# Five edits to the order of a macaron block's kernel: branches, bias splits, a scheduling fence, placement sums and the attention's instruction order

## The chip, the cores and the metric

The kernel runs on one core of a Trainium2 chip. A core has TensorE (PE, with its weight loads listed as PEld), VectorE (DVE), ScalarE (ACT), GpSimd (POOL) and SyncE (SP), which work side by side and wait for each other by semaphores; DMA queues are fed by SP, ACT and POOL. The metric is the device time of one launch in microseconds (us); lower is better.

## The reference

All data is fp32; `x` is (4, 1024, 256). A block of three residual parts is computed:

```python
x = x + 0.5 * ffn(layernorm(x))
x = x + attn(layernorm(x))      # 16 heads; k and v from a 128-wide latent; rope; mask by pages of 64
x = x + 0.5 * ffn(layernorm(x)) # the same weights again

def fff(x, nw, nb, w1, b1, w2, b2, act):      # 256 leaves of width 16, tree of depth 8
    node = 0
    for _ in range(8):
        node = 2 * node + 1 + ((x . nw[node]) + nb[node] > 0)
    leaf = node - 255
    return act(x @ w1[leaf] + b1[leaf]) @ w2[leaf] + b2[leaf]

def ffn(x):
    xn = (x - mean(x)) / sqrt(std(x) + 1e-5)
    q, k, v = (fff(xn, ..., relu) for each of three weight sets)
    y = xn + softmax(q k^T / sqrt(256)) v      # one head, per batch of 1024 tokens
    return y + fff(y, ..., gelu)               # the fourth set, f
```

So each ffn holds four fast feed-forward trees (q, k, v, f) and a single-head attention between v and f.

## The kernel before, in words

The 4096 tokens are 32 tiles of 128. A tree goes through these steps. **Routing** (`route`, `routes`): PE transposes tiles of `xn` (L317), multiplies with all node weights (L326), DVE compares with thresholds `thr` (`bits`, L334), and PE and ACT turn the bits into one-hot leaves. **Placement** (`place`, `ranks`, `blocks_ended`): the 256 leaves form 32 blocks of 8. A token's slot in a list sorted by block is worked out, each block padded to whole tiles; `blocks_ended` adds up how many tiles each block has with small matmuls, L439, L447 and L465, with short DVE chains between them. **Scatter** (`scattering`, `go`): POOL writes each token's row to its slot in DRAM, one indirect DMA a tile (L554). **Build** (`load_first`): a w1 load `raw` is transposed on PE (L615) and copied to its tile by ACT (L620) and DVE (L618, half of the pieces for q, k and v). **Leaves** (`leaves`): for each of up to 63 tiles SP loads 128 sorted rows `xg` (L656); PE transposes them (L662), multiplies with its block's w1 (L680), adds the bias by a matmul with `b1p` (L683), DVE masks the leaf (L688), PE transposes again (L698) and multiplies with w2 (L705). The first 48 tiles are always done; the rest stand behind three nested run-time branches in `spare_leaves` (L641), which each engine takes by itself.

`b1p` is the bias b1 in three bf16 parts. `load_raw` loads b1 three times on SP's queue (L589) ahead of the w1 loads, and `split_b1` makes the parts with seven DVE operations: one copy (L597), three subtractions (L601) and three copies (L602). Both are called once for each tree in each ffn.

Side work is written as generators, which `with_steps`, `beside` or the due times (`at`, `due`) of the single-head attention move on, one step after each leaf tile, routing group or score step. k is placed beside q's leaves and v beside k's leaves. f is routed and placed beside the single-head attention, in three runs of tiles (`in_runs`, called by `place_run(k, n)` for n steps of run k), and its rows are settled there (L1055). q's placement is drained in one go.

A scheduler of the framework orders each engine's instructions by its own estimate of when they are ready, except inside `in_order()`, where they stay in source order. `tc.keep_in_program_order` pins single DMAs. The w2 load of v is issued on ACT's queue (L572) behind k's branches, which no instruction is moved across, and v's w1 is built right behind it; then `coming` gathers rows of k and q (`y_k` and `b_k`, POOL, L739 and L753), DVE adds them (L972) and PE turns them, beside v's leaves.

The 16-head attention runs 16 units of 12 steps (four batches by four groups of heads). A step has two waves: in each, two heads' scores for the maxima (L1403, reduced by DVE, L1410) and two heads' scores for the weights (L1437, exponentials on ACT, L1444); the weighted sums are L1455. All the scores share a few PSUM banks `big`. Between them, `prepare` makes the next tiles' q, k and v: z (DVE, L1358), its transposes (PE, L288), the latent (L1365), q and k (L1373, L1379), rope on DVE (L1291, L1293) and POOL (L1296, L1298), v's copy `vpad` (ACT, L1381), and the transposes of q and k by heads (L1304) with their copies `qTh` and `kTh` (L1383, L1385). The whole of it is in source order:

```python
es.enter_context(in_order())
```

Of the kernel before, what the change touches and what calls it, by code (L numbers as in the profile page):

```python
# [71 lines left out]
def macaron_kernel(ctx: ExitStack, tc: tile.TileContext, a: dict, out: bass.AP):  # L72
# [33 lines left out]
    def sm(shape):  # L106
        return bank("sm", shape)
# [37 lines left out]
    null = const.tile([P, 1], F32, name="null")  # L145

# [287 lines left out]
    def blocks_ended(pool, acc, t, last=True, k=0, before=()):  # L434
# [11 lines left out]
        pe = sm([NBLK, 1])  # L446
        nc.tensor.matmul(pe, tri[:NBLK, :NBLK], upto[:, :1], start=True, stop=(k == 0))  # L447
        if k:
            nc.tensor.matmul(pe, ones[:NBLK, :NBLK], before[1], start=False, stop=True)
# [5 lines left out]
        nc.vector.tensor_copy(upto[:, 1:], total)  # L455
        end = pool.tile([NBLK, 1], F32, name=f"endc{k}", tag=f"endc{k}")
# [3 lines left out]
        if last:  # L460
            nc.vector.tensor_scalar(past, tiles, end, None, ALU.is_ge)
        else:
            nc.vector.tensor_scalar(past, tiles, end, null[:NBLK], ALU.is_ge, ALU.mult)
        pg = sm([P, GCOL])
        nc.tensor.matmul(pg, ones[:NBLK], past, start=True, stop=True)  # L465
        return pg, (total, upto[:, 1:])
# [10 lines left out]
    def place(pool, oh, acc, rows, gblk, sel):  # L477
# [10 lines left out]
        n, _ = blocks_ended(pool, acc, NT)  # L488
        yield
        tile_blocks(pool, n, end, gblk, sel)  # L490
# [3 lines left out]
    def in_runs(pool, oh, acc, rows, gblk, sel):  # L494
# [9 lines left out]
        def run(k):  # L504
# [30 lines left out]
            n, before = blocks_ended(pool, acc, hi, last, k, before)  # L535
# [49 lines left out]
    def load_raw(pool, f):  # L585

        b1 = pool.tile([3 * NBLK, P], F32, name=f"b1_{FFFS[f]}", tag="b1")
        for k in range(3):
            nc.sync.dma_start(  # L589
                b1[k * NBLK : (k + 1) * NBLK, :],  # L590
                a[f"{FFFS[f]}_b1"].rearrange("(b e) l -> b (e l)", e=EPB),
            )
        return b1, [load_part(pool, f, *p) for p in PART[:2]]

    def split_b1(b1p, b1):

        nc.vector.tensor_copy(b1p, b1)  # L597
        for k in range(1, 3):
            for q in range(k, 3):
                one = slice(q * NBLK, (q + 1) * NBLK)  # L600
                nc.vector.tensor_sub(b1[one], b1[one], b1p[one])  # L601
                nc.vector.tensor_copy(b1p[one], b1[one])  # L602
# [25 lines left out]
    def spare_leaves(*what):  # L628
# [12 lines left out]
        with ExitStack() as es:  # L641
            for lo, hi in zip(SPARE, SPARE[1:]):
                es.enter_context(tc.If(used > lo))
# [155 lines left out]
    def ffn(first: bool, last: bool):  # L799
# [13 lines left out]
        with ExitStack() as es:  # L813
            xn = stage(es, "xnp", 1).tile([P, NT, E + 2], F32, name="xn")
            idx = stage(es, "idx", 1)
            slot, leaf, gblk, sel, b1p = [], [], [], [], []
            for nm in FFFS:
# [4 lines left out]
                b1p.append(idx.tile([3 * NBLK, P], BF16, name=f"b1p_{nm}"))  # L822
# [17 lines left out]
            with ExitStack() as ws, banks(0, 8):  # L840
# [8 lines left out]
                with ExitStack() as hs, ExitStack() as rs:  # L849
                    raw = stage(rs, "raw", 1, "right")  # L850
                    pp = stage(hs, "place", 1)
                    with ExitStack() as rt:
# [38 lines left out]
                        b1, ahead = load_raw(raw, 0)  # L891
                        split_b1(b1p[0], b1)
# [17 lines left out]
                        b1, ahead = load_raw(raw, 1)  # L910
# [10 lines left out]
                        split_b1(b1p[1], b1)  # L921
# [15 lines left out]
                    b1, ahead = load_raw(raw, 2)  # L937
# [12 lines left out]
                    split_b1(b1p[2], b1)  # L950
                    drain(load_first(raw, 2, w1, ahead))

# [54 lines left out]
            b1, raws = load_raw(raw, 3)  # L1007
            with in_order(), qs, ExitStack() as ats, banks(2, 4):
# [169 lines left out]
                drain(weights)  # L1178
                path = route(rp, 3, NT - 1, *hot_f, leaf[3], 1)
# [4 lines left out]
            with ExitStack() as fs, banks(0, 8):  # L1184
                with in_order():
# [53 lines left out]
    def attention():  # L1239
# [7 lines left out]
        with ExitStack() as es:  # L1247
# [73 lines left out]
            es.enter_context(in_order())  # L1321
# [318 lines left out]
```

## Time and profile before

| what | value |
|---|---|
| times of three runs | 2679.99, 2681.26, 2692.75 us; median 2681.26 |
| the profiled execution | 2683.48 us, span 2681.6 us |
| mean granted TensorE clock | 0.952 of full |
| busy share of the span | PE 88%, PEld 56%, DVE 55%, ACT 40%, POOL 32% |
| start and routing of q, first ffn | 0 to 75 us |
| scatter and build of q, routing of k | 75 to 147 us |
| leaves of q; build of k and routing of v | 147 to 222; 222 to 262 us |
| leaves of k; build of v; leaves of v | 262 to 355; 355 to 378; 378 to 470 us |
| single-head attention, then f | 470 to 800; 800 to 897 us |
| 16-head attention | 897 to 1790 us |
| second ffn | 1790 to 2682 us |

The profile page has one execution on the chip. A row of waits reads: engine, tile and line that stood idle, then the engine (or DMA), tile and line that ended the wait, then total us, number of times, and the longest. A row of the timeline reads: start, duration, engine, line, operation, tiles out<-in with sizes, and in brackets the engine's idle time before it and what ended that. A row of one line's instructions ends in shortest/median/longest ns; a q behind an engine's name is its sequencer. Windows give busy times, granted clock and the share of the DMA engines for a stretch of the span. Bounds of the stages above are read from such windows.

### The profile page before, as it was taken

What the parts mean: (1) busy time and instruction counts of PE and PEld (TensorE: products, weight loads), DVE (VectorE), ACT (ScalarE), POOL (GpSimd) and SP (SyncE); (2) the same over time, 40 slices, a digit from 0 to 9 for tenths busy, and PEclk for the clock granted to TensorE, in tenths of its full rate; (3) what the DMA queues carried; (4) which work ended last, traced back from release to release, by engine and by line L of the source; (5) the groups of instructions that cost most, each with busy time, mean ns of one, the idle gap of its engine ahead of it and who ended that gap; (6) DMA issues with size and microseconds to landing.
All of it is one profiled execution on the core that took longest, in us unless ns stands there. A gap on an engine that the chain in (4) does not pass through costs nothing. (4 is left out here: it accounts for less than half of the span.)

```text
span 2681.6 us, 43134 instructions
## 1 busy us (share of the span) xinstructions
PE 2364.6 (88%) x14388; PEld 1511.0 (56%) x14430; DVE 1483.1 (55%) x4401; ACT 1064.1 (40%) x2491; POOL 855.1 (32%) x978
## 2 busy tenths in 40 slices
PE   7789878999988679999999999979999899999874
PEld 3476777566657434434344344435676785666573
DVE  8554544455545475666665667645645454455453
ACT  3334344233224224545554545544443452332241
POOL 0431344466445311101101100003421554664453
PEclk9889989999998779999999999999999899999987
DMA  9966686344226200000000000002656873442265
GB/s 284 334 199 214 205 247 194 123 147 145 66 103 211 89 8 1 1 1 1 1 1 1 1 1 1 2 33 95 227 186 222 267 231 123 144 144 69 97 204 167
DMA packets 236919, 321.22 MB, mean 120 GB/s; under 512 B 28529, under 2 KB 208002, under 8 KB 232584
## 3 DMA queue, kind: packets, MB, share of 16 engines
q1 hardware_dynamic: 150480, 170.24, 20.7%
q0 software_dynamic: 38640, 100.90, 11.9%
q10 hardware_dynamic: 47560, 47.06, 5.4%
q8 instruction: 130, 2.13, 0.3%
q14 instruction: 109, 0.89, 0.1%
HBM read 193.59 MB, written 129.33 MB: 120 GB/s over the span
## 5 line engine op out<-in xcount | busy, mean ns | idle before, releaser
L1410 DVE TENSOR_REDUCE mxh<-big 128x1 f32<-128x512 f32 (+3 forms) x768 | 391.9, 552 | 251.0 <-PE big L1403 248.4
L1444 ACT ACTIVATE pTh<-big 128x512 f32<-128x512 f32 (+3 forms) x768 | 332.7, 489 | 287.8 <-PE big L1403 257.3
L1403 PE MATMUL big<-kTh,qTh 32*128 32x512 f32 (+3 forms) x1536 | 407.3, 541 | 7.7 <-DVE mxh L1410 6.1
L1437 PE MATMUL big<-qTh,kTh 32*128 32x512 f32 (+3 forms) x1536 | 342.5, 534 | 0.1
L326 PE MATMUL sm<-xT,nwT 128*128 128x512 f32 (+2 forms) x528 | 240.1, 598 | 10.1 <-DVE bits L334 7.3
L767 PE MATMUL two<-kT,qT 128*128 128x512 f32 x512 | 237.3, 608 | 10.0 <-ACT pr L780 8.4
L688 DVE SCALAR_TENSOR_TENSOR hm<-eid,xg,sm 128x128 f32<-128x128 f32 x399 | 138.1, 346 | 187.0 <-PE sm L683 185.5
L795 PE MATMUL sm<-vb,pT 128*128 128x256 f32 x1024 | 232.0, 380 | 1.8 <-DVE pT L791 1.8
L707 ACT COPY og<-sm 128x256 f32<-128x256 f32 x399 | 148.7, 373 | 151.4 <-DMA ytok<-og,tok 39.2
L795 PEld LDWEIGHTS sm<-vb,pT 128*128 128x128 f32 x1024 | 190.0, 190 | 28.2 <-DVE pT L791 3.5
L700 ACT ACTIVATE hid<-sm 128x128 f32<-128x128 f32 x399 | 111.3, 279 | 229.0 <-PE sm L698 227.5
L1437 PEld LDWEIGHTS big<-qTh,kTh 32*128 32x128 f32 x1536 | 115.9, 184 | 148.2 <-issue 72.9
L662 PE MATMUL sm<-ident,xg 128*128 128x128 f32 x798 | 161.3, 286 | 25.8 <-DMA xg<-xs_f 18.3
L1403 PEld LDWEIGHTS big<-kTh,qTh 32*128 32x128 f32 x1536 | 156.1, 185 | 42.5 <-ACT pTh L1444 23.4
L664 DVE COPY xgT<-sm 128x256 f32<-128x256 f32 x399 | 166.4, 417 | 21.0 <-PE sm L662 20.1
L1455 PE MATMUL sm<-pTh,vpad 128*32 128x512 f32 (+3 forms) x1536 | 167.3, 499 | 4.7 <-ACT pTh L1444 4.7
L334 DVE TENSOR_SCALAR bits<-sm,thr 128x512 bf16<-128x512 f32 (+1 forms) x132 | 96.8, 734 | 121.7 <-PE sm L326 121.0
L326 PEld LDWEIGHTS sm<-xT,nwT 128*128 128x128 f32 x528 | 98.4, 196 | 114.7 <-issue 87.8
L767 PEld LDWEIGHTS two<-kT,qT 128*128 128x128 f32 x512 | 95.1, 195 | 110.3 <-issue 97.3
L320 ACT COPY xT<-sm 128x512 f32<-128x512 f32 (+1 forms) x130 | 69.7, 582 | 198.7 <-PE sm L317 198.3
L775 DVE TENSOR_REDUCE mx<-two 128x1 f32<-128x1024 f32 x64 | 78.3, 1224 | 125.2 <-PE two L767 125.2
L1419 POOL TENSOR_SCALAR mpad<-mxh 128x16 f32<-128x16 f32 x32 | 8.9, 279 | 390.0 <-DVE mxh L1410 234.8
(322 smaller groups left out, 4413.6 us busy)
## 6 DMA issues: line engine op xcount, KB each, us to landing
xg<-xs SPq DMA_DIRECT2D x298, 128.5 KB
xs<-zero SPq DMA_DIRECT2D x2, 8095.5 KB
xs_f<-zero ACTq DMA_DIRECT2D x14, 1032.0 KB
xg<-xs_f SPq DMA_DIRECT2D x101, 129.0 KB
os_q<-og SPq DMA_DIRECT2D x101, 128.0 KB
os_v<-og SPq DMA_DIRECT2D x101, 128.0 KB
os_k<-og SPq DMA_DIRECT2D x96, 128.0 KB
raw_q<-in_q_w SPq DMA_DIRECT2D x8, 1024.0 KB
```

The lines of the kernel that those rows point to most:

```text
L326: nc.tensor.matmul(pl, nwT[:, c, f, r * P : (r + 1) * P], xT[:, c, :], start=(c == 0), stop=(c == KC - 1),)
L662: nc.tensor.transpose(pa[:, c, :], xg[:, x0 + c * P : x0 + (c + 1) * P], ident)
L664: nc.vector.tensor_copy(xT, pa)
L688: nc.vector.scalar_tensor_tensor(hm, eid, xg[:, lf : lf + 1], ph, ALU.is_equal, ALU.mult)
L707: nc.scalar.copy(og, po)
L767: nc.tensor.matmul(ps[:, n0 : n0 + 512], qT[:, c, i * P : (i + 1) * P], kT[:, c, n0 : n0 + 512], start=(c == 0), stop=(c == KC - 1),)
L795: nc.tensor.matmul(po, pT[:, j, :], vb[:, j, :], start=(j == 0), stop=(j == TPB - 1))
L1403: nc.tensor.matmul(ps[:, :n], qT[r : r + HPAD, hg, i * P : (i + 1) * P], kT[r : r + HPAD, hg, n0 : n0 + n], start=True, stop=True,)
L1410: nc.vector.tensor_reduce(maxima(b, hg)[:, i, c, u : u + 1], ps[:, :n], AX.X, ALU.max)
L1437: nc.tensor.matmul(ps[:, off:], kT[r : r + HPAD, hg, j * P : (j + 1) * P], qT[r : r + HPAD, hg, qb * QN + off : (qb + 1) * QN], start=True ...
L1444: nc.scalar.activation(pT[:, u, off:], ps[:, off:], AF.Exp, scale=1.0 / math.sqrt(HD))
L1455: nc.tensor.matmul(acc[r : r + HPAD, off:], vpads[b % 2][:, j, 4 * hg + 2 * pair + u, :], pTs[pair][:, u, off:], start=(j == 0), stop=(j = ...
```

## The change

There are five edits.

1. `spare_leaves` tells the compiler that the block without work comes next behind the compare. In the program, the small block of the case "not taken" now lies directly behind the compare, and the bodies behind it; before, the bodies came first.
2. b1 is loaded on ACT's queue, and only in the first ffn; its parts `b1p` are kept in the constants for both. The splits are written beside k's routing; the scheduler puts all 28 operations and the 12 loads into q's routing (loads of b_q ahead of and among the `thr` loads, b_k behind them, b_v and b_f among ACT's work at about 45 and 56 us of the old profile).
3. `tc.no_sync_barrier()` behind v's build: the scheduler may not move instructions across that place; nothing waits for it at run time. On DVE the copies of `w_v` now come ahead of the first three adds L972, and on POOL gathers of `y_k` and `b_k` alternate.
4. `blocks_ended` becomes a generator that pauses ahead of each of its two later matmuls, and the calls of `place_run` are spread to match. L447 and L465 of k, v and f come behind a leaf tile, a score step or a build step.
5. In the 16-head attention source order ends with the first unit of 12 steps; the scheduler orders the rest. On PE the score matmuls L1437 come ahead of the transposes of z (L288) in 21 cases; on DVE z (L1358) moves up to 32 reduces earlier; on ACT the copy `vpad` moves behind one or two exponentials in 24 of 32 prepares; on POOL the copies L1298 come ahead of the additions L1296.

The number of instructions on PE and POOL does not change. The diff, with four hunks that only rename left out:

```diff
@@ -143,6 +143,8 @@
 mod32 = const.tile([P, 1], F32, name="mod32")
 null = const.tile([P, 1], F32, name="null")
+b1p = [const.tile([3 * NBLK, P], BF16, name=f"b1p_{nm}") for nm in FFFS]
 with tc.tile_pool(name="nodes", bufs=2) as np_, banks(0, 8):
     nc.vector.memset(nwT[:, :, :, NODES:], 0.0)
@@ -431,7 +433,7 @@
     nc.vector.tensor_scalar_mul(first, first, float(P))
     return first
-def blocks_ended(pool, acc, t, last=True, k=0, before=()):
+def blocks_ended(pool, acc, t, found, last=True, k=0, before=()):
@@ -443,16 +445,17 @@
 ng = tiles_of(pool, n)
 upto = pool.tile([NBLK, 2], BF16, name=f"upto{k}", tag=f"upto{k}")
 nc.vector.tensor_copy(upto[:, :1], ng)
-pe = sm([NBLK, 1])
-nc.tensor.matmul(pe, tri[:NBLK, :NBLK], upto[:, :1], start=True, stop=(k == 0))
-if k:
-    nc.tensor.matmul(pe, ones[:NBLK, :NBLK], before[1], start=False, stop=True)
 total = pool.tile([NBLK, 1], F32, name=f"total{k}", tag=f"total{k}")
...
 nc.vector.tensor_copy(upto[:, 1:], total)
+yield
+pe = sm([NBLK, 1])
+nc.tensor.matmul(pe, tri[:NBLK, :NBLK], upto[:, :1], start=True, stop=(k == 0))
+if k:
+    nc.tensor.matmul(pe, ones[:NBLK, :NBLK], before[1], start=False, stop=True)
 end = pool.tile([NBLK, 1], F32, name=f"endc{k}", tag=f"endc{k}")
 nc.vector.tensor_add(end, pe, ng)
 past = pool.tile([NBLK, GCOL], BF16, name="past_g", tag="past_g")
@@ -461,9 +464,10 @@
         nc.vector.tensor_scalar(past, tiles, end, None, ALU.is_ge)
     else:
         nc.vector.tensor_scalar(past, tiles, end, null[:NBLK], ALU.is_ge, ALU.mult)
+    yield
     pg = sm([P, GCOL])
     nc.tensor.matmul(pg, ones[:NBLK], past, start=True, stop=True)
-    return pg, (total, upto[:, 1:])
+    found += [pg, (total, upto[:, 1:])]
 def tile_blocks(pool, n, end, gblk, sel):
@@ -485,9 +489,10 @@
     for h in range(2):
         yield from ranks(pool, oh, acc, rows, h * NT // 2, (h + 1) * NT // 2, first)
         yield
-    n, _ = blocks_ended(pool, acc, NT)
+    found = []
+    yield from blocks_ended(pool, acc, NT, found)
     yield
-    tile_blocks(pool, n, end, gblk, sel)
+    tile_blocks(pool, found[0], end, gblk, sel)
 RUNS = (0, NT - TPB, NT - GT, NT)
@@ -532,7 +537,9 @@
         pass
     yield
 last = k + 2 == len(RUNS)
-n, before = blocks_ended(pool, acc, hi, last, k, before)
+found = []
+yield from blocks_ended(pool, acc, hi, found, last, k, before)
+n, before = found
 yield
 if k:
     nc.vector.tensor_add(ended, ended, n)
@@ -584,22 +591,24 @@
 def load_raw(pool, f):
-    b1 = pool.tile([3 * NBLK, P], F32, name=f"b1_{FFFS[f]}", tag="b1")
+    return [load_part(pool, f, *p) for p in PART[:2]]
+def load_b1(pool, f):
+    b1 = pool.tile([3 * NBLK, P], F32, name=f"b1_{FFFS[f]}", tag="b1", bufs=2)
     for k in range(3):
-        nc.sync.dma_start(
+        nc.scalar.dma_start(
             b1[k * NBLK : (k + 1) * NBLK, :],
             a[f"{FFFS[f]}_b1"].rearrange("(b e) l -> b (e l)", e=EPB),
         )
-    return b1, [load_part(pool, f, *p) for p in PART[:2]]
-def split_b1(b1p, b1):
-    nc.vector.tensor_copy(b1p, b1)
+    yield
+    nc.vector.tensor_copy(b1p[f], b1)
     for k in range(1, 3):
         for q in range(k, 3):
             one = slice(q * NBLK, (q + 1) * NBLK)
-            nc.vector.tensor_sub(b1[one], b1[one], b1p[one])
-            nc.vector.tensor_copy(b1p[one], b1[one])
+            nc.vector.tensor_sub(b1[one], b1[one], b1p[f][one])
+            nc.vector.tensor_copy(b1p[f][one], b1[one])
+        yield
 def load_first(pool, f, w1, raws, on_both=True):
@@ -640,7 +649,7 @@
 )
 with ExitStack() as es:
     for lo, hi in zip(SPARE, SPARE[1:]):
-        es.enter_context(tc.If(used > lo))
+        es.enter_context(tc.If(used > lo, preferred_fallthrough_block=False))
         for _ in leaves(*what, lo, hi):
             pass
@@ -888,8 +896,7 @@
 if first:
     clear(nc.sync, xs[0])
 w1 = w1_of(0)
-b1, ahead = load_raw(raw, 0)
-split_b1(b1p[0], b1)
+ahead = load_raw(raw, 0)
 if first:
     tc.keep_in_program_order(clear(nc.sync, xs[1]))
 build = load_first(raw, 0, w1, ahead)
@@ -898,16 +905,28 @@
 going = scattering(0, slot[0], rows, 5)
 hot = hots_of(pp, 1, 2)
+if first:
+    b1s = [load_b1(raw, f) for f in range(len(FFFS))]
+    for g in b1s[:2]:
+        next(g)
 def beside(k):
     drain(islice(build, 3 * (k > 0)), islice(going, 1))
+    if first and k and k % 2 == 0:
+        f = k // 2 - 1
+        drain(b1s[f])
+        if f + 2 < len(FFFS):
+            next(b1s[f + 2])
 routes(hp, 1, *hot, leaf[1], beside)
 drain(build, going)
+if first:
+    drain(*b1s)
 w2 = load_second(nc.sync, wp, 0)
...
 what = tree(0, AF.Relu, w1, w2)
-b1, ahead = load_raw(raw, 1)
+ahead = load_raw(raw, 1)
 rows = []
 with_steps(
     leaves(*what),
@@ -947,8 +965,8 @@
         tc.keep_in_program_order(clear(nc.sync, osrt[2][SPARE[0] * P :]))
     w1 = w1_of(2)
     w2 = load_second(nc.scalar, wp, 2)
-    split_b1(b1p[2], b1)
     drain(load_first(raw, 2, w1, ahead))
+    tc.no_sync_barrier()
 early = stage(ws, "early", 2)
 head = stage(qs, "qk", 1, "right")
@@ -1074,7 +1092,6 @@
 def number():
     nc.vector.tensor_scalar_add(xn[:, :, E + 1], cst[:, C_JC : C_JC + NT], pid)
-    split_b1(b1p[3], b1)
 def clear_some(k):
@@ -1118,11 +1135,12 @@
     t = 8 * (step - 27)
     for where, ts in enumerate((range(t, t + 2), range(t + 2, t + 5), range(t + 5, t + 8))):
         at(step, where, go, *ts)
-at(28, 2, place_run, 0, 1)
-at(29, 2, place_run, 0, 9)
+for step, where in ((28, 0), (28, 1), (29, 0), (29, 1)):
+    at(step, where, place_run, 0, 1)
 at(30, 2, place_run, 1, 2)
 at(30, 2, go, *range(RUNS[1], RUNS[2]))
-at(31, 2, place_run, 1, 9)
+for where in range(3):
+    at(31, where, place_run, 1, 1)
 def routing(t):
@@ -1176,6 +1194,7 @@
 weights = begin_weights()
 next(before)
 drain(weights)
+place_run(1, 9)
 path = route(rp, 3, NT - 1, *hot_f, leaf[3], 1)
 for g in (before, path, before, path):
     next(g)
@@ -1200,9 +1219,12 @@
 last_b2(*range(NT - GT, NT))
 w2 = load_second(nc.scalar, wp, 3)
 place_run(2, 1)
-drain(islice(build, 4))
+drain(islice(build, 3))
 place_run(2, 1)
 go(*range(RUNS[2], NT))
+for _ in range(3):
+    place_run(2, 1)
+    drain(islice(build, 2))
 drain(build)
 place_run(2, 9)
 settled(*range(NT - TPB, NT))
@@ -1318,7 +1340,8 @@
     nc.scalar.activation(r, r, AF.Sqrt)
     nc.vector.reciprocal(r, r)
-es.enter_context(in_order())
+beginning = ExitStack()
+beginning.enter_context(in_order())
 def arriving(ends, ahead, queue):
@@ -1529,6 +1552,8 @@
 prep, made = chain(*[prepare(0, i) for i in range(TPB)]), 0
 for n in range(len(units) * UNIT + LAG):
     first = n < UNIT
+    if n == UNIT:
+        beginning.close()
     if n % (4 * UNIT) == LAG + 1 and n // (4 * UNIT) + 1 < B:
         b = n // (4 * UNIT) + 1
         prep = chain(*[prepare(b, i) for i in range(TPB)])
```

More of the change, by code (lines that the diff above doesn't have):

```diff
@@ L815, in ffn @@
             idx = stage(es, "idx", 1)
-            slot, leaf, gblk, sel, b1p = [], [], [], [], []
+            slot, leaf, gblk, sel = [], [], [], []
             for nm in FFFS:
@@ L821, in ffn @@
                 sel.append(idx.tile([3 * NBLK, GCOL], BF16, name=f"sel_{nm}"))
-                b1p.append(idx.tile([3 * NBLK, P], BF16, name=f"b1p_{nm}"))
             def hots_of(pool, f, bufs):
@@ L920, in ffn @@
                         w1 = w1_of(1)
-                        split_b1(b1p[1], b1)
                         build = load_first(raw, 1, w1, ahead)
@@ L936, in ffn @@
                     what = tree(1, AF.Relu, w1, w2)
-                    b1, ahead = load_raw(raw, 2)
+                    ahead = load_raw(raw, 2)
                     ahead += [load_part(raw2, 2, *p) for p in PART[2:]]
@@ L1006, in ffn @@
             hot_f = hots_of(stage(rs, "hot_f", 1), 3, 1)
-            b1, raws = load_raw(raw, 3)
+            raws = load_raw(raw, 3)
             with in_order(), qs, ExitStack() as ats, banks(2, 4):
```

## The prediction

> **What bounds the kernel now.** I read the page first. TensorE (PE) is busy 88% of a span of 2681.6 us at a granted clock of 0.952, and no other engine passes 55%:
>
> ```profile
> PE 2364.6 (88%) x14388; PEld 1511.0 (56%) x14430; DVE 1483.1 (55%) x4401; ACT 1064.1 (40%) x2491; POOL 855.1 (32%) x978
> ```
>
> So time comes from two places: PE's idle gaps, and the slow clock after long gaps. Next I read what PE waited for over the whole span (total us, times, longest):
>
> ```profile
> PE sm L288 <- DVE z L1358: 35.2, 18, 13.7
> PE sm L662 <- DMA xg<-xs_f: 18.3, 2, 9.9
> PE sm L447 <- DVE total L454: 15.3, 8, 4.4
> PE sm L615 <- DVE w_v L618: 12.1, 4, 6.9
> PE sm L326 <- DVE bits L334: 7.3, 1, 7.3
> PE sm L465 <- DVE past_g L461: 6.0, 8, 1.4
> PE sm L1304 <- ACT vpad L1381: 4.9, 10, 1.6
> PE sm L447 <- DVE upto L445: 4.3, 4, 1.2
> PE sm L465 <- DVE past_g L463: 2.3, 4, 0.6
> ```
>
> Lines 447 and 465 are the placement sums, 615 is v's build, 326 is k's routing, 288 and 1304 are attention. Each belongs to one part of the change.
>
> **Sums a step apart.** The four rows of 447 and 465 make 15.3 + 6.0 + 4.3 + 2.3 = 27.9 us. Windows over the stages split them: q's two sums (1.3 + 1.4 and 1.5 + 1.4 = 5.6) are drained at once in both kernels and stay. The last run of f (0.94 + 0.63 and about as much again, 3.0) lies inside PE's wait for f's first gather (8.4 and 9.9 us, row L662), so covering it gains nothing. Left are k and v (four times 0.92 + 0.52 = 5.7), f's first run (twice 4.42 + 0.58 = 10.0) and second (twice 1.23 + 0.57 = 3.6): 19.3 us. PE now does a leaf tile or a score step in between; I found those long enough, since 8 + 8 + 8 transposes and scores take 1.04 + 3.60 + 1.04 = 5.7 us against about 5 us of DVE chain. The 4.42 us gap also costs clock: behind it eight L790 take 1.97 us and eight L767 5.24, undisturbed 1.04 and 3.60. That is 2.6 us, and 2.4 in the second FFN: 5.0. Sum **24.3**. The moved steps also hold back POOL's scatter of k, v and f by some 2.5 us; k's and v's have over 20 us to spare. Lower bound 12: the eight L1055 adds (3.5 us, now behind the sums on DVE) could hold the next pT copy, and the clock might not recover. Upper bound 27.9.
>
> **A fence behind v's w1.** The timeline of the first FFN shows the stall, and behind it what will be late next:
>
> ```profile
> 358.50 0.39 ACTq L572 DMA_DIRECT2D w_v<-in_v_w  x1
> 366.61 0.43 DVE L972 TENSOR_TENSOR y_k<-y_k,b_k 128x256 f32<-128x256 f32 x1 [13.29 <-DMA y_k<-os_k,slot_k]
> 368.71 3.59 DVE L618 COPY w_v<-sm 128x512 f32<-128x512 f32 x4
> 369.77 2.63 PE L615 MATMUL sm<-ident,raw_v 128*128 128x128 f32 x11 [4.65 <-DVE w_v L618]
> 380.13 0.60 PE L705 MATMUL sm<-w_v,hid 128*128 x2
> ```
>
> DVE stood 13.29 us at an add that needs gathered rows, with w_v's copies queued behind it; PE lost 4.65 us here and 6.92 in the second FFN. In the new order the copies come first and both gaps go, 11.6 us. But the first row starts the 4 MB load of w2 that L705 reads. Its 4096 packets run 359.6 to 379.4 us with the DMA engines full (share 1.04), and 2117.7 to 2136.9; the first L705 stood at 380.13 and 2140.85. So no more than 0.7 + 3.9 = **4.6** us can come out; w2 is the next late thing. Cost: the three prefetches of b_k move behind gathers on POOL, 3.8 us there; POOL is 43% busy in that stage. Bounds 1 and 11.6 (if w2 lands as much earlier).
>
> **b1 split once, on ACT's queue.** DVE stands at the split of b_v:
>
> ```profile
> 131.51 0.22 DVE L597 CAST b1p_v<-b_v 96x128 bf16<-96x128 f32 x1 [11.31 <-DMA b_v<-in_v_b]
> 133.70 2.93 PE L326 MATMUL sm<-xT,nwT 128*128 128x512 f32 x3 [7.28 <-DVE bits L334]
> ```
>
> Its loads sat on SP behind a clear that held the queue 15.5 us. They go, so the 7.28 us go; next late would be q's gathered rows, landed by 136 us against a first use at 147. The clock was 0.50 from 130 to 138 us, where 4.3 us of PE work took twice its time: 2.0 more. Against it: two loads of b_q stand ahead of the thresholds on ACT, 2 x 0.43 = 0.9 us, and DVE already waits 4.1 us for those; three split operations (0.22 + 0.28 + 0.22 = 0.7) fall before PE's first routing matmul, when PE waits for DVE; the other 18 or so new ones make 4.6 us where DVE is idle only 6.0 us of 40 (windows 26 to 66), of which I put 1.4 on the path. Six more loads on ACT at 45 to 57 us (2.6 us) lie beside a half idle ACT. SP's other stalls (27 and 20 us behind a clear) pass to the next load and stay. In the second FFN 28 operations of 0.25 us go from beside a busy PE: nothing, with 0.2 at most where xn waits. Net 7.3 + 2.0 - 3.0 = **6.3**. Bounds: -3 (b_v and b_f are needed some 4 us after issue, and DVE would stand there with the DMA engines full) and +9.
>
> **Fall-through of the branches.** It moves blocks, not work; instruction counts are the same. Not taken, PE now falls into its small block and then jumps far, where it jumped far first and then fell through. The row for the compare (shortest/median/longest ns):
>
> ```profile
> L641 PEldq COMPARE_BRANCH  x14: 70/334/3654, 222.9 to 2649.3; - x14
> ```
>
> Three of the 14 last 2.95 to 3.65 us, the rest 0.07 to 0.35. One far jump per FFN remains, so I take **0**, bounds 7 us to either side (two of those stalls). [...]
>
> **Source order in one attention unit only.** From the second unit on the scheduler orders the engines. Three moves matter. z (L1358) goes 30 reduces ahead on DVE; two of four score matmuls go ahead of z's transposes; vpad's copy falls behind one exponential, in five prepares behind two. What PE sees before:
>
> ```profile
> 1238.19 0.63 PE L1304 MATMUL sm<-ident,qpad 128*128 128x128 f32 x4 [0.39 <-ACT vpad L1381]
> 1242.68 0.59 ACT L1385 COPY kTh<-sm 128x512 f32<-128x512 f32 x1
> 1243.44 0.41 PE L288 MATMUL sm<-ident,z 128*128 128x128 f32 x2 [1.01 <-DVE z L1358]
> ```
>
> The gap before z stands 24 times, 26.6 us in all. With z early the same bank still waits for the kTh copy: where that was last the gap is 0.68 us, so 24 x 0.68 = 16.3 stay unless score work covers it. But scores run four at once on PE's row groups; two sent ahead take as long as four, so they cover nothing that isn't paid later. Gain 10.3. Against it, vpad later by a 0.55 us exponential in 13 prepares that already wait at L1304 or stand within 0.04 us of it, and by a second in five: 10 us. I take **0**, bounds 26.6 gained and 20 lost.
>
> **The sum.** 24.3 + 4.6 + 6.3 + 0 + 0 = 35.2 us off the profiled execution of 2683.48: 2648.3. That execution lies 2.2 above the median of the runs, 2681.26, so I say **2646**. What a measurement can tell from no change is about 0.5%, 13.4 us: under 2667.9 is faster.
>
> **Rivals.** (1) The attention order helps: transposes and scores interleave without loss and the z gaps close, 16 to 26 us more, about 2626. For it: PE's only regular gap there is this one. Against it: vpad's row. Chance 0.12. (2) The covers are thin: f's first run gives back its 10.0 and its clock 5.0 as a wait at L795 for pT, and b1's early cost eats its 6.3; 21 us, about 2667. For it: DVE is the chain in both places. Chance 0.18, half of it past the bound. (3) Slower: in attention, L1403 and L1437 begin to wait for a score bank. Units 2 to 16 have 15 x 12 x 2 = 360 waves; it decides from (35 + 13) / 360 = 0.13 us each, a quarter of a 0.55 us reduce or exponential. At 0.2 us it is 72 us, about 2718. Against it: DVE is busy 65% and ACT 51% there, and L1403 waited 0.8 us for its bank from 1000 to 1400. Chance 0.08. (4) The far jumps really go: three stalls on PE, 9 us, 2637. Against it: the jump that remains. Chance 0.07. My own case, 0.55, spans 2634 to 2660.
>
> **How the numbers follow.** Faster: 0.55 + 0.12 + 0.07 and a bit over a third of (2), 0.80; same: the rest of (2), 0.12; slower 0.08. The range takes in case (1) with its 26 at the lower end and (2) with w2's bound at the upper: 2624 to 2674; outside are (3) and half of the extremes.
>
> **What would show it.** In the new profile: 447 and 465 left with about 8 us, q's and f's last run alone; L767 back to 3.60 behind f's first run; no wait of L615 for w_v, but L705 (or L680) waiting for w_v's load, first L705 hardly earlier after v's fence in the first FFN; b1 gone from 120 to 134 us and q's leaves 7 us earlier relative to q's sums; compares of 3 to 3.65 us replaced by branches as long; z's row at L288 gone, kTh and vpad in its place. I am wrong if the stretch from 1000 to 1795 us changes by over 10 us, or if the first 75 us grow by more than 4.

## The result, and the profile after

The changed kernel takes 2661.10 us (median of 7 runs, 2653.55 to 2670.55) against 2681.26 for the kernel before (7 runs beside it): ratio 0.9922 with a 95% interval of 0.9895 to 0.9948, so 20.2 us less. That is inside the range of 2624 to 2674, and 15 us short of the forecast of 2646. The profiled execution took 2664.47 us, with a span of 2662.6 and a granted clock of 0.956 (0.952 before). Line numbers are the new program's; the old L615, L680, L705 and L972 are L624, L689, L714 and L990.

The page's row of PE:

```profile
PE 2390.1 (90%) x14388; PEld 1519.5 (57%) x14430; DVE 1478.2 (56%) x4373; ACT 1063.1 (40%) x2491; POOL 856.1 (32%) x978
```

The span fell by 19 us while PE's busy time rose by 25.5 us with the same 14388 matmuls. So about 44 us of idle time went, and more than half of it came back as time in which PE is listed as busy. What PE waits for over the span (total us, times, longest):

```profile
PE sm L290 <- DVE z L1381: 19.5, 7, 11.7
PE sm L1326 <- POOL kpad L1318: 11.8, 13, 1.0
PE sm L689 <- DVE xgT L673: 11.2, 7, 5.3
PE sm L671 <- DMA xg<-xs_f: 9.7, 2, 5.5
PE sm L456 <- DVE upto L447: 8.5, 3, 3.6
PE sm L456 <- DVE total L452: 4.5, 5, 1.5
PE sm L319 <- issue: 4.2, 1, 4.2
PE sm L624 <- DVE w_v L627: 3.0, 6, 1.1
```

In the same view of the kernel before, the wait for `xgT` was:

```profile
PE sm L680 <- DVE xgT L664: 4.9, 7, 1.0
```

The waits for `w_v`, `bits` and most of `z` are gone or smaller, as are those for the placement sums (the rows of L456 and L469 make 17.2 us, 27.9 before; 5.7 of it are q's). New are L689 waiting for `xgT` (4.9 before, 11.2 now) and L1326 waiting for `kpad`. The stages, from starts of PE's matmuls (us): the leaves of q, k and f run from their first matmul with w1, those of v from their first with w2, all to their last with w2; the single-head attention ends with its last score, and a build or a start is what lies between.

| stage | before, 1st / 2nd ffn | after, 1st / 2nd ffn | difference |
|---|---|---|---|
| start to q's leaves | 151.2 / 135.3 | 144.5 / 133.4 | -6.7 / -1.9 |
| leaves of q | 71.7 / 80.5 | 70.9 / 80.3 | -0.8 / -0.3 |
| routing of v, build of k | 61.0 / 57.4 | 62.8 / 56.4 | +1.7 / -1.0 |
| leaves of k | 70.5 / 69.7 | 69.8 / 68.1 | -0.7 / -1.7 |
| build of v | 25.7 / 26.4 | 24.3 / 24.5 | -1.4 / -2.0 |
| leaves of v | 90.4 / 72.2 | 93.3 / 77.4 | +2.9 / +5.2 |
| single-head attention | 310.4 / 312.2 | 305.2 / 303.7 | -5.2 / -8.5 |
| build of f, first rows | 40.7 / 42.1 | 39.4 / 41.1 | -1.3 / -1.0 |
| leaves of f | 66.6 / 79.0 | 68.9 / 78.6 | +2.3 / -0.4 |
| from f's leaves to the first score of the 16 heads | 25.2 | 23.6 | -1.6 |
| 16-head attention, first to last score | 858.1 | 861.0 | +2.9 |

Two rows show what the prediction had wrong: v's leaves lost more than v's build won, and the 16-head attention got longer although its waits shrank.

### The profile page after: what moved, and what is told of

Its sections match the earlier page's. It is cut to its first block, busy times and chain, and to the rows that moved or that the text cites. A ratio compares the mean times of both kernels' runs of the same rounds, so it can differ in the third digit from the quotient of the medians.

```text
span 2662.6 us, 43062 instructions
## 1 busy us (share of the span) xinstructions
PE 2390.1 (90%) x14388; PEld 1519.5 (57%) x14430; DVE 1478.2 (56%) x4373; ACT 1063.1 (40%) x2491; POOL 856.1 (32%) x978
## 5 line engine op out<-in xcount | busy, mean ns | idle before, releaser
L1426 PE MATMUL big<-kTh,qTh 32*128 32x512 f32 (+3 forms) x1536 | 405.8, 542 | 7.7 <-DVE mxh L1433 6.1
L1460 PE MATMUL big<-qTh,kTh 32*128 32x512 f32 (+3 forms) x1536 | 354.4, 533 | 0.1
L1460 PEld LDWEIGHTS big<-qTh,kTh 32*128 32x128 f32 x1536 | 118.9, 184 | 150.0 <-DVE mxh L1433 76.3
L1426 PEld LDWEIGHTS big<-kTh,qTh 32*128 32x128 f32 x1536 | 151.3, 186 | 48.6 <-ACT pTh L1467 27.6
L784 DVE TENSOR_REDUCE mx<-two 128x1 f32<-128x1024 f32 x64 | 78.3, 1223 | 117.3 <-PE two L776 117.1
L707 PE MATMUL sm<-ident,hm 128*128 128x128 f32 x399 | 112.9, 283 | 19.7 <-DVE hm L697 19.6
```

The lines of the kernel that those rows point to most:

```text
L1426: nc.tensor.matmul(ps[:, :n], qT[r : r + HPAD, hg, i * P : (i + 1) * P], kT[r : r + HPAD, hg, n0 : n0 + n], start=True, stop=True,)
L1460: nc.tensor.matmul(ps[:, off:], kT[r : r + HPAD, hg, j * P : (j + 1) * P], qT[r : r + HPAD, hg, qb * QN + off : (qb + 1) * QN], start=True ...
```

## The experiments

Single executions of one kernel differ by up to 25 us, so the ratios carry intervals. Runs of one set share a chip and the runs of the kernel before, whose median was 2692.74 in the first set, 2694.99 in the second and 2910.37 in the third; times of different sets are not compared. First set: `after_again`, `x_attn_in_order`, `x_no_fence`, `x_sums_at_once`; second: `x_fence_prefetch`, `x_z_ahead`, `x_b1_twice`, `x_no_fallthrough`; third: the last four.

**The changed kernel again**, as the base of the first set.

> The changed kernel once more, as the yardstick for the three beside it: 19 to 21 us below the kernel before, a ratio of 0.992. Every other run of this set is read against this one.

Measured: 2669.47, ratio 0.9924 (0.9894 to 0.9953). The gain repeats.

**The sums drained at once again** (edit 4 undone):

```diff
-        yield
         pe = sm([NBLK, 1])
...
-        yield
         pg = sm([P, GCOL])
...
-                for step, where in ((28, 0), (28, 1), (29, 0), (29, 1)):
-                    at(step, where, place_run, 0, 1)
+                at(28, 2, place_run, 0, 1)
+                at(29, 2, place_run, 0, 9)
```

> The placement sums drained at once as before, all else as in the changed kernel. Theory (q's and f's last run hidden or unchanged, the rest covered, and the clock dip behind the 4.42 us gap gone): 13 to 20 us slower than the changed kernel, with gaps of 4.4 us at L447 in both single-head attentions and eight L767 behind them at over 5 us. The prediction's term says 24. Rival (covers are thin, most of it comes back as other waits): under 6 us slower.

Measured: 2690.21, ratio 0.9987 (0.9970 to 1.0004): nearly all of the gain is gone. The edit is worth about 0.9987 - 0.9924 = 0.0063, 17 us (some 9 to either side). The single-head attention takes 311.1 and 311.5 us, 305.7 and 304.6 with the edit. f's first run in this kernel, on PE's timeline, and then in the changed one:

```profile
753.85 0.17 PE L449 MATMUL sm<-upto,tri 32*32 32x1 bf16 x1 [4.42 <-DVE total L456]
754.60 0.23 PE L467 MATMUL sm<-past_g,ones 32*128 32x64 bf16 x1 [0.58 <-DVE past_g L465]
```

```profile
739.94 0.17 PE L456 MATMUL sm<-upto,tri 32*32 32x1 bf16 x1
...
744.57 0.20 PE L469 MATMUL sm<-past_g,ones 32*128 32x64 bf16 x1
744.69 3.70 PE L776 MATMUL two<-kT,qT 128*128 128x512 f32 x8
```

In the second, no idle time in brackets stands behind the sums: the DVE chain runs beside the matmuls between them, and the eight score matmuls behind take 3.70 us, not 5.24.

**Without the fence** (edit 3 undone):

```diff
-                    tc.no_sync_barrier()
```

> Without the fence behind v's w1, all else as in the changed kernel. Theory (the fence keeps b_k's three gathers from being issued early, the first adds then hold xgT on DVE, and w2's 4 MB load caps what is won before the first L705): 2 to 6 us faster than the changed kernel; v's build longer by 3 to 4 us in the two ffns together, v's leaves shorter by 6 to 9. Rival (the prediction's term): 4.6 us slower. Second rival: within 1.5 us, since w2's load sets the start of v's leaves in both.

Measured: 2663.15, ratio 0.9894 (0.9872 to 0.9916), about 8 us less than with the fence; the two intervals overlap. The stages are clearer: build and leaves of v take 25.0 + 87.8 and 26.9 + 72.1 us, against 26.2 + 91.5 and 23.9 + 78.7 in the changed kernel beside it, 8.6 less in sum. In the first profiles and the first two sets these stages take 219.4 to 223.7 us in all eight kernels with the fence, and 211.7 (this one) and 214.7 (the kernel before) without it. The fence costs time here, which the prediction had excluded. The changed kernel's timeline at the end of v's build, second ffn, in its first profile:

```profile
2115.56 0.40 DVE L990 TENSOR_TENSOR y_k<-y_k,b_k 128x256 f32<-128x256 f32 x1
2117.10 0.43 DVE L990 TENSOR_TENSOR y_k<-y_k,b_k 128x256 f32<-128x256 f32 x1 [1.14 <-DMA b_k<-in_k_b,leaf_k]
2119.60 0.42 DVE L990 TENSOR_TENSOR y_k<-y_k,b_k 128x256 f32<-128x256 f32 x1 [2.07 <-DMA b_k<-in_k_b,leaf_k]
2120.51 1.20 PE L689 MATMUL sm<-w_v,xgT 128*128 x4 [5.34 <-DVE xgT L673]
2126.18 1.19 PE L714 MATMUL sm<-w_v,hid 128*128 x2 [0.74 <-DMA w_v<-in_v_w]
```

`w_v`'s copies are done, but the three adds did not vanish: they now stand ahead of the copy of `xgT`, the first leaf's rows, and wait for rows of `b_k` whose gathers the fence moved behind it and set between those of `y_k` and `vb`. The stall passed from L624 to L689. Behind it the granted clock is 0.50 while the leaves' dense work begins; without the fence PE stands idle for 9.09 us in the build itself, up to 2120.59, and the clock of 0.50 falls on the transposes of w1. Windows of that stretch in the changed kernel and then without the fence (the columns are us, then busy us with counts of PE, PEld, DVE, ACT and POOL, granted clock, DMA share, GB/s):

```profile
2119.00:2121.00 2.00, 0.49 (x2) 0.53 (x3) 1.09 (x3) 0.00 (x0) 1.63 (x2) 0.72 1.11 359
2121.00:2123.00 2.00, 2.00 (x13) 1.88 (x12) 0.77 (x2) 0.00 (x0) 1.46 (x2) 0.50 1.05 342
2123.00:2125.00 2.00, 2.00 (x12) 1.94 (x11) 0.94 (x3) 0.28 (x1) 1.39 (x2) 0.50 0.83 277
2125.00:2127.00 2.00, 1.26 (x5) 0.80 (x4) 0.61 (x2) 0.28 (x1) 1.69 (x2) 0.50 0.39 108
2127.00:2129.00 2.00, 2.00 (x11) 1.85 (x11) 0.56 (x2) 0.37 (x1) 1.15 (x2) 0.50 0.88 252
2129.00:2131.00 2.00, 2.00 (x13) 1.81 (x12) 0.43 (x2) 1.02 (x3) 0.95 (x1) 0.72 0.79 227
```

```profile
2114.00:2116.00 2.00, 0.00 (x0) 0.00 (x0) 0.00 (x0) 0.00 (x0) 0.00 (x0) 0.81 1.09 359
...
2120.00:2122.00 2.00, 1.41 (x7) 1.27 (x8) 2.00 (x3) 0.25 (x1) 1.62 (x2) 0.50 1.09 348
2122.00:2124.00 2.00, 2.00 (x11) 1.60 (x9) 1.97 (x3) 1.29 (x2) 1.39 (x3) 0.50 1.09 357
2124.00:2126.00 2.00, 1.75 (x11) 1.32 (x10) 1.01 (x1) 1.30 (x2) 1.70 (x2) 0.63 0.77 239
2126.00:2128.00 2.00, 1.46 (x14) 1.22 (x12) 1.85 (x3) 1.22 (x2) 1.39 (x3) 1.00 0.28 84
```

With the fence PE works some 9 us at a clock of 0.50, without it some 5, which costs about 2 us more. DVE's masks `hm` are later too: L707 waits 7.1 us in the rest of v's leaves, 4.5 without the fence:

```profile
PE sm L707 <- DVE hm L697: 7.1, 7, 2.7
```

```profile
PE sm L707 <- DVE hm L697: 4.5, 7, 0.9
```

These two, 2 + 2.6, are most of the 5.3 us by which v's leaves differ in the second ffn between these two profiles; this split is read from the rows, and no run separates it.

**Source order all through the 16-head attention** (edit 5 undone):

```diff
-            beginning = ExitStack()
-            beginning.enter_context(in_order())
+            es.enter_context(in_order())
```

> The whole 16-head attention in source order again, all else as in the changed kernel. Theory (idle was turned into busy time: the z gaps closed by 22.7 us, but the score matmuls that were sent ahead no longer run four at once, PE busy +19.7 us in the units, and qpad's waits grew by 7.5): 1 to 4 us faster than the changed kernel, PE busy time of L1437 (before's numbering) back from 354 to 342 us. Rival (the scheduler's order gains, and the 2.9 us by which the units were longer are chance): 5 to 15 us slower.

Measured: 2670.44, ratio 0.9916 (0.9888 to 0.9943), the same as the changed kernel. From first to last score it takes 856.8 us against 860.2 (860.1 and 861.2 in the set's other two kernels with edit 5). On the third set's chip no such difference shows: 859.3 in source order, 860.2 and 857.4 with edit 5. Two windows over nearly all of this attention, in the kernel before and then in the changed one, from the first profiles (770 and 774 us long, columns as above):

```profile
1001.00:1771.00 770.00, 729.86 (x5372) 312.77 (x5372) 473.42 (x1072) 397.68 (x937) 55.81 (x127) 0.99 0.00 1
```

```profile
990.00:1764.00 774.00, 749.59 (x5380) 316.14 (x5376) 477.44 (x1075) 398.02 (x940) 58.08 (x127) 1.00 0.00 1
```

PE is idle 40.1 us in the first and 24.4 in the second, and busy 19.7 us longer for nearly the same matmuls (5372 and 5380). The groups of the weights' scores, in the changed kernel and with source order all through (matmuls, busy us, mean ns of one):

```profile
L1460 PE MATMUL big<-qTh,kTh 32*128 32x512 f32 (+3 forms) x1536 | 354.4, 533 | 0.1
```

```profile
L1459 PE MATMUL big<-qTh,kTh 32*128 32x512 f32 (+3 forms) x1536 | 342.0, 533 | 0.1
```

One matmul lasts 533 ns in both, 1536 x 533 ns is 819 us, and busy time is what they cover together: they overlap less, 819 / 354.4 = 2.31 deep instead of 2.39, and this group alone is busy 12.4 us longer. Sending two of four scores ahead of z's transposes fills the gap with work that then lacks its neighbours: in the changed kernel's profile four L1460 of 32x256 take 0.70 us alone ahead of z's transposes (from 1249.57), and four of L1460 with four of L1426, of the same size, take 0.72 together (from 1252.95).

**z one tile ahead, in source order** (edit 5 undone, and z issued by hand a tile early, its transposes one step later):

```diff
+                if b and i + 1 < TPB:
+                    zs[t + 1] = normed(t + 1)
...
+                if b:
+                    yield
```

> The whole 16-head attention in source order, with z written one tile earlier (behind the rope of q) and a step put between the transposes of kpad and those of the next z, from the second batch on; so four score matmuls still start together. All else as in the changed kernel. Theory (the gap at z can be closed without splitting the scores): the 18 to 22 us that PE stood before z go, PE busy time of the scores stays at 342 us, and the units from first to last score take 836 to 845 us against 857 to 858 in source order and 860 to 861 in the changed kernel; 15 to 22 us faster than the changed kernel, ratio about 0.985. Rival (the bank rotation moves the wait to the next transposes or to vpad): the units at 852 or more, 3 to 8 us faster only.

Measured: 842.8 us from first to last score, 13.8 less than the mean of the three kernels with edit 5 in the same set (856.0, 855.7, 858.2). The scores stay together (345.1 us busy, 536 ns of one), and the waits of nearly the same stretch are, with z ahead and then with plain source order:

```profile
PE sm L1326 <- ACT vpad L1412: 7.0, 6, 1.6
PE sm L290 <- DVE z L1376: 1.8, 1, 1.8
```

```profile
PE sm L290 <- DVE z L1380: 14.2, 12, 1.3
```

So the gap before z can be closed without splitting the scores. The whole kernel took 2670.87, ratio 0.9897 (0.9865 to 0.9930); that it beats the changed kernel as a whole is likely and not shown.

**b1 split in both ffns** (edit 2 undone: b1 on SP's queue, `split_b1` called for each tree):

```diff
-            nc.scalar.dma_start(
+            nc.sync.dma_start(
...
-                        ahead = load_raw(raw, 0)
+                        b1, ahead = load_raw(raw, 0)
+                        split_b1(b1p[0], b1)
```

> b1 loaded on SP's queue and split for each ffn as before, all else as in the changed kernel. Theory (the 7.28 us wait of k's routing for the bits, behind the split of b_v, and the slow clock with it): 4 to 8 us slower than the changed kernel, nearly all of it before q's first leaf. Rival (the gathers of q's rows and the clears fill the DMA engines until then anyway, on a chip where they are a little slower): within 2 us.

Measured: 2684.79, ratio 0.9949 (0.9925 to 0.9972). The start takes 160.6 us, 155.7 to 157.1 in the other three of the set, so the edit gives 3.5 to 4.9 us there. The wait that it takes away is back, in DVE's row and in PE's:

```profile
141.63 0.22 DVE L602 CAST b1p_v<-b_v 96x128 bf16<-96x128 f32 x1 [9.75 <-DMA b_v<-in_v_b]
```

```profile
PE sm L326 <- DVE bits L334: 5.7, 1, 5.7
```

In the changed kernel the wait for `b_v` has not gone; part of it stands in q's routing instead. Its first profile:

```profile
45.63 1.32 ACTq L600 DMA_DIRECT2D b_v<-in_v_b  x3
55.73 0.22 DVE L605 CAST b1p_v<-b_v 96x128 bf16<-96x128 f32 x1 [4.98 <-DMA b_v<-in_v_b]
57.38 5.40 PE L328 MATMUL sm<-xT,nwT 128*128 128x512 f32 x8 [2.07 <-ACT xT L322]
82.86 0.16 PE L456 MATMUL sm<-upto,tri 32*32 32x1 bf16 x1 [1.43 <-DVE total L452]
```

DVE stands 4.98 us at the split, ACT behind it, and PE then waits 2.07 us for `xT`; the eight matmuls that follow take 5.40 us, 3.70 in the group before them. The kernel before has no such wait, and its first sum of q is earlier:

```profile
78.25 0.16 PE L447 MATMUL sm<-upto,tri 32*32 32x1 bf16 x1 [1.34 <-DVE total L454]
```

In the profiles of all eleven kernels with edit 2 PE's longest wait for `xT` in q's routing is 1.9 to 2.5 us, and 0.7 in the three without it. On the third set's chip the edit gains nothing at the start: the kernel with the fence alone takes 152.0 us to q's leaves, the three with edit 2 take 155.1 to 156.1.

**Plain branches** (edit 1 undone):

```diff
-                es.enter_context(tc.If(used > lo, preferred_fallthrough_block=False))
+                es.enter_context(tc.If(used > lo))
```

> The branches without the preferred fall-through, all else as in the changed kernel. Theory (one far jump remains in each order): within 2 us of the changed kernel, and PE's longest stalls at the branches of 3 to 4 us in both, at the compare here and behind the unconditional branch there. [...]

Measured: 2676.71, ratio 0.9932 (0.9906 to 0.9957), no difference. Its waits show the two long stalls under the branch's own line:

```profile
PE sm L319 <- PEq L650: 4.3, 1, 4.3
PE sm L624 <- PEq L650: 3.3, 1, 3.3
```

In the changed kernel they stand as "issue", 4.2 us at L319 and 4.4 the longest at L624. On PE's sequencer its profile has a row of L650 of 0.10 us at 215.4 and one of 3.67 at 216.1, and 0.08 at 348.0 and 3.88 at 348.6; the kernel before has single rows of 3.65 us at 222.9 and 3.50 at 354.5. So the compare became short, and a second branch behind it is as long as the compare was.

**The prefetch of b_k ahead of the fence.** If the lost prefetch is the whole reason, three gathers put ahead of the fence bring the gain.

```diff
-                    tc.no_sync_barrier()
...
                 early = stage(ws, "early", 2)
+                b2_k = [fetch_b2(early, 1, t, leaf[1], 3, "") for t in range(3)]
+                tc.no_sync_barrier()
```

> The fence is kept, but put behind three gathers of b_k that stand ahead of it, so that they are issued during k's leaves as in the kernel before; all else as in the changed kernel. Theory A (the lost prefetch is what the fence cost: the adds held xgT 5.3 us in the second ffn): PE's wait for xgT at v's start under 1.5 us in both ffns, v's leaves of the second ffn back from 77 to 79 us to 72 to 74, ratio at or under the 0.989 of the kernel without the fence. Theory B (w2's load and the cold clock behind the stall set it, wherever the stall is): xgT's wait goes, a wait of L705 for w_v of 3 us or more takes its place, v's leaves stay near 77, ratio within 0.001 of the changed kernel's 0.992.

Measured: 2677.69, ratio 0.9918 (0.9887 to 0.9949), no gain; v's leaves take 95.4 and 78.3 us. PE's longest wait at the end of v's build in the second ffn:

```profile
PE sm L714 <- DMA w_v<-in_v_w: 4.7, 1, 4.7
```

With the adds early, L689 waits no more than 1.8 us for `xgT`, and w2 is late by 4.7 (4.4 in the first ffn). Two things end at nearly the same time here, the adds and the load.

**The fence alone, on the kernel before.**

```diff
+                    tc.no_sync_barrier()
```

> The kernel before with the fence behind v's w1 and nothing else. Theory (the stall moves from v's build to the wait for w2 and the first leaves, which then run at the slow clock): v's builds 1 to 2.5 us shorter, v's leaves 3 to 7 longer, in each ffn; 3 to 9 us slower than the kernel before, ratio 1.001 to 1.0035. Rival (the prediction's term): 4.6 us faster, ratio 0.998.

Measured: 2898.95, ratio 0.9961 (0.9941 to 0.9982): faster by 11 us, against the expectation. No profile of the kernel before was taken on this chip, so the stage that gained isn't shown. The next two kernels and the last point to one, k's leaves.

**Without v's w2 load**: v's leaves multiply with k's w2, so that part of the computation is changed.

```diff
-                    w2 = load_second(nc.scalar, wp, 2)
```

> The changed kernel without the load of v's w2: v's leaves use k's w2 that is still in place, so 4 MB less are loaded in each ffn. Theory (w2's load is what is late next behind the fence): the first L705 stands 17 to 21 us behind the last of k's instead of 24, no wait for w_v; v's leaves of the second ffn at 72 to 75 us as without the fence, since the clock does not fall. Rival (the adds on DVE and the gathers set it): first L705 at 23 us or later, waits for xgT and hm as before, v's leaves at 76 or more.

> The same without the fence. Theory: with nothing else late, DVE's wait at the adds shows in full: first L705 at 22 to 26 us behind the last of k's, 4 to 7 us later than in the kernel with the fence, which is the gain that the prediction would have had. Rival: no difference beyond 1.5 us.

Measured with the fence: 2866.47, ratio 0.9849 (0.9813 to 0.9886); v's build 24.7 and 23.8 us, leaves 98.7 and 82.9. Without fence and load: 2872.34, ratio 0.9860 (0.9819 to 0.9900); build 28.7 and 27.4, leaves 87.4 and 75.4. The build with the fence does not fall to the 17 to 21 us of the theory that w2 sets it; with the fence alone, and the load, it takes 25.4 and 24.0. Build and leaves together take 123.4 and 106.7 us with the fence, 116.0 and 102.8 without: v's leaves are longer behind a fence here too, and that is not for w2's load. But k's leaves, just ahead, go the other way: 78.2 and 78.1 us with the fence, 84.5 and 79.8 without. From k's first leaf to v's last it is 386.3 against 383.1 us, and the two ratios do not differ.

**No fence, z ahead, the rest as changed**, the version that the first two sets point to:

> What the runs point to: b1 split once, the sums a step apart, no fence, the 16-head attention in source order with z one tile ahead and a step between kpad's and z's transposes. From the kernel without the fence (0.9894) less 15 to 18 us in the units: ratio 0.982 to 0.985, about 45 us under the kernel before. If the two do not add up, 0.988.

Measured: 2876.87, ratio 0.9883 (0.9852 to 0.9914), and 845.0 us for the 16-head scores. The attention's gain is there. But v's build takes 34.1 and 33.7 us, about 8 more than without the fence in the first set, from two waits in the first ffn:

```profile
PE sm L624 <- DVE w_v L627: 10.5, 2, 10.2
PE sm L689 <- DVE xgT L673: 6.8, 1, 6.8
```

DVE's longest waits for `y_k`, in front of `w_v`'s copies, are 12.7 and 13.0 us, no longer than the 12.2 and 13.9 without the fence in the first set; why PE waits longer behind them is open. The gain of the fence alone is not in v's stages either: its build and leaves take 233.5 us in the two ffns together, 231.5 here. The difference is in k's leaves, 78.5 and 77.9 us with the fence alone and 83.8 and 82.1 here. The last part of k's leaves in the first ffn, without w2's load, with the fence and then without it (columns as above):

```profile
356.80:375.00 18.20, 15.90 (x114) 13.99 (x114) 8.37 (x30) 8.39 (x28) 5.76 (x6) 1.00 0.63 199
```

```profile
355.00:379.50 24.50, 18.73 (x116) 15.90 (x114) 8.30 (x29) 8.37 (x28) 8.88 (x10) 0.86 0.55 166
```

Without the fence the three gathers of `b_k` lie here, and the clock is lower (0.86 against 1.00). From k's first leaf to v's last it is 389.8 us with the fence alone and 397.3 here. That fits the 11 us which the fence alone gained, and does not prove it; why k's leaves lengthen on this chip is open, and in the first set they do not clearly (67.3 and 70.1 us without the fence; 67.6 and 66.0, 69.5 and 68.8 in two kernels with it). Whether this version beats the changed kernel is not shown.

## Why the prediction was right or wrong

**Branches: right.** Predicted 0, measured no difference. The 4.2 and 4.4 us waits of the changed kernel stand in place of 4.3 and 3.3 with plain branches, and the second branch there lasts 3.67 and 3.88 us, where the compare of the kernel before lasted 3.65 and 3.50. What that time goes to is not shown.

**b1: right in the sum, by two errors that cancel.** 6.3 predicted; the start shrank by 6.7 in the first profiles and by 3.5 to 4.9 in the second set. The feared cost ahead of the first routing matmul did not show: PE's longest wait for `xn` went from 12.2 to 11.6 us. But the prediction's own sign of being wrong, the first 75 us growing by more than 4, did: q's first sum starts 4.6 us later (82.86 against 78.25), as DVE stands at the split of b_v. The prediction had named this as its lower bound and put 3.0 into the sum for all costs. From that sum to q's leaves 11.3 us went instead of 9.3. That the total came out is in part luck, and on the third set's chip it did not.

**Sums: right in kind, too large by some 5 to 7 us.** 24.3 predicted; about 17 by the ratios, and the stages agree: -13.7 in the single-head attention, -3.5 in the leaves of q and k, and -2.3 in f's build, which the forecast left out. Of the 19.3 us of idle time all but about 3 went. f's last run now waits 3.6 + 1.4 and 3.5 us, but the wait for f's first rows fell from 18.3 to 9.7 in return: the step that called that run hidden was right. The mis-sized term is the clock's 5.0: the rows of the sums lost 6.8 and 5.4 us of idle time in the two single-head attentions, 12.2, and the stages gained 13.7, so 1.5 is left for the clock. It came in the second ffn (8.5 gained, 3.1 more than the rows lost) and not in the first (5.2, 1.6 less), although there the eight matmuls behind the first run are nearly as fast as forecast (3.70 us, 3.60 undisturbed); what took it back is open. With the 3 us of idle time that stayed, 24.3 becomes 18.

**Fence: wrong, with the sign.** This is the step that failed. The prediction let 4.6 us come out and gave bounds of 1 and 11.6, with no loss. It wrote that "the copies come first and both gaps go", and followed only what stood behind the adds. It did not ask what the adds, now later, stand in front of: the copy of `xgT`. It also costed the three moved gathers of `b_k` by POOL's busy share, 3.8 us on an engine at 43%, where what counts is when the row lands that an add waits for (1.14 and 2.07 us behind the fence in the second ffn). In the first set the fence costs 8.6 us in v's build and leaves, 4.8 in the first profiles; with the 4.6 that were forecast that is 9.4 us of what is missing. The named next limit, w2, was right as far as it went: it appears as soon as the adds are early, as a wait of 4.7 us. Taking away either alone brings little: with the adds early the ratio stays at 0.9918, and without w2's load v's build and leaves take 230.0 us in the two ffns together, 233.5 with the fence alone on that chip. Both at once wasn't tried, so which rows set v's leaves behind the fence is shown in part only. The third set's `x_fence_only` says that the sign for the whole kernel is not the same on every chip: there v's leaves are longer behind the fence too, and k's leaves, which the prediction did not look at, are shorter.

**Attention: right in the end, by another balance, so partly by luck.** 0 predicted as 10.3 - 10, measured +2.9 us in the first profiles and +3.4 in the first set. PE's idle time did fall by 15.7 us, and `vpad`'s wait did not grow: L1326 waits for `kpad` instead, 11.8 us in 13 cases. What gave the rest back is the loss of overlap among the scores (2.31 deep instead of 2.39, 12.4 us in the group of the weights' scores). The prediction named it ("two sent ahead take as long as four, so they cover nothing that isn't paid later"), yet priced only the idle gaps.

Between the two profiled executions 19.0 us went, where the sum of 35.2 was forecast: 16.2 are missing. The fence makes 9.4 of them, the sums 7.1 (24.3 against 17.2 in the single-head attention and the leaves of q and k), the attention 2.9. k's build and f's leaves grew by 0.7 and 1.9 over the two ffns; against this go f's build (2.3), the start of the second ffn (1.9) and the stretch ahead of the first score (1.6). For these five the prediction had nothing. f's build gained as f's first rows came earlier; the causes of the other four are not shown.

## What to carry to other kernels

When a reorder puts work B ahead of a stalled A, look at what A is now in front of, and at every transfer that A waits for: a stall that is not removed at its source moves to the next consumer, as here the adds' wait moved to `xgT` (5.34 us in the second ffn) and part of the wait for `b_v` to q's routing (4.98 us on DVE, 2.07 on PE). A gap on an engine that runs several small matmuls side by side is not free time (here PE was idle 15.7 us less in the 16-head attention and busy 19.7 us longer): judge a new order there by the stage's length, not by its idle time. And where two limits end together (here the adds and w2), one edit against either brings little (with the adds early the ratio was 0.9918, and PE waited 4.7 us for w2's load).

## What the runs showed of the hardware

- PE's busy time can grow at the same number and mean duration of matmuls, when 32-row matmuls lose their neighbours: 1536 of them cover 354.4 us instead of 342.0 (depth 2.39 to 2.31). Over the attention PE was busy 19.7 us longer and idle 15.7 us less, and nothing was won.
- The granted clock was 0.50 for some 10.2 us at the end of v's build in the second ffn, with the fence (0.72 in the windows 2119 to 2121 and 2129 to 2131, 0.50 between) and without it (0.81 in 2114 to 2116, 0.63 in 2124 to 2126, 0.50 between). By these windows the clock fell at about 2119.9 and 2115.2 us. What differs is how soon PE was back at work: at 2120.51, 0.6 us later, with the fence, and at 2120.59, some 5.4 us later, without. With the fence PE was busy throughout the windows from 2127 to 2131, behind the wait of 0.74 us that ended at 2126.18, and the clock was 1.00 again from 2131. What brings the clock back is not shown: no run here varies that wait.
- A chip on which the kernel before takes 2910 us instead of 2693 runs the 16-head attention in the same time (859.3 us from first to last score with the fence alone, 858.1 for the kernel before in its first profile); the single-head attention of the first ffn takes 367 to 372 us in the four kernels there, 304 to 311 in the others. What slows that stage was not found.
